# A four-layer graph kernel: the length-1 LSTM of 1024 tokens as seven block products, and the pieces of the neighbouring streams placed anew

## The chip, the cores and the metric

The kernel runs on one core of a Trainium2 chip. The metric is the device time of one launch in microseconds (us). An execution under the profiler gives the trace and the page that are read here. The engines are named as in the profile: PE (TensorE, matmuls), PEld (its weight loads), DVE (VectorE), ACT (ScalarE), POOL (GpSimd) and SP (SyncE, which only issues DMAs here). Each engine has its own instruction stream; they meet through semaphores.

## The reference, cut to what matters

128 graphs of 64 nodes with 256 channels go through four layers, each with a residual. The layer that matters here is the second: two graph convolutions, and then LSTMs over windows of the 64 nodes of length 1, 2, 3 and 4, one after the other, each of which writes the last state of every window back into `h`.

```python
h = relu(einsum('ts,bsh->bth', adj, x @ Wg0 + bg0))
h = relu(einsum('ts,bsh->bth', adj, h @ Wg1 + bg1))
for p in range(1, 5):
    nw = 64 // p
    wins = h[:, :nw * p].reshape(Bv * nw, p, 256)
    last = lstm_last(Wih[p - 1], Whh[p - 1], bih[p - 1], bhh[p - 1], wins)   # gates i, f, g, o; zero initial state
    h = h.at[:, arange(nw) * p + p - 1].set(last.reshape(Bv, nw, 256))
```

With length 1 every token is a window of its own. The state starts at zero, so the forget gate and `Whh` drop out: i, g and o are `x @ Wih.T + bias`, the cell is sigmoid(i) * tanh(g), the state sigmoid(o) * tanh(cell).

## The kernel before, in words

The 8192 tokens are 16 chunks of 512. Stage 1 and stage 2 (layer 1) go over the chunks; then comes the LSTM stage, then layers 3 and 4. The LSTM stage has 8 **rounds** (`sc`) of two chunks, so of 1024 tokens. The data of a round is `hT`, channels on the partitions: 2 blocks of 128 channels by 64 nodes by 16 graphs.

A matmul is [128 x 128] weights by [128 x n] data into one PSUM bank of 512 f32 per partition. During the LSTM stage there are 8 banks: two each of the tags x, y and z, and two (ps) for other work (`banks_of("psum1", x=2, y=2, z=2, ps=2)`).

`lstm(p, hv, sets, name)` (L1009) does one length. For p = 1 it is called twice a round with 512 tokens each: 3 gates x 2 channel blocks x 2 input blocks = 12 matmuls of 512 columns (L1123), weights `wih1`. ACT reads the banks directly (`first_acts`, L1102: sigmoid or tanh with bias), DVE multiplies the cell (`first_cell`, L1108) and writes the states (L1062). For p = 2 to 4 the first step is the same kind of product (L1123; for p = 2, in rounds 1 to 7, in two sets of 256 columns, since the two halves of the tokens become ready one after the other). The later steps are done per gate by **seven block products** instead of eight (class `Unit`, L1159): with the 2 x 2 blocks of the weights and the two halves of the tokens, kinds 1 to 7 are products of sums and differences, which are then added up. Sums of weights lie in the `wset` tiles, loaded from `wfar` in memory, where `weight_sums` put them during stage 2. Differences of the data are made by `differences` (L313 to L316), on POOL for the inputs (`xd`), on DVE for the states (`hd`). Kinds 1, 6, 7 and 4 add up in one x bank, each being read on the way: after kind 1 ACT copies the bank (L1165), only then may kind 6 be added into it. Kind 5 goes to a y bank and is copied too; kinds 2 and 3 go to z.

The order of the work is written out by hand: in the LSTM stage the program order is the order of the instructions on all five engines (`manual_schedule`). The LSTM is a Python generator that yields at 22 **places** in a round, 0 to 21, and at each place pieces of other streams are emitted:

- Places 0 to 3 lie in length 1, 4 to 7 in length 2, 8 to 13 in length 3, 14 to 21 in length 4. In lengths 2 to 4 the first place lies between the two input blocks of the first product, the second after the first products of the next step (kinds 5, 3, 2 from x) and just ahead of kind 5 from h, its copy, kind 1, its copy, kinds 3, 6, 2; then come two per step, in its middle and at its end. Place 17 is the end of a step of length 4 and, like place 9, lies just ahead of those products and copies.
- `convolutions(c)` (14 steps) prepares a chunk of the next round. Step 1: scale on DVE, two transposes on DVE, a put to memory, a read-back, and the load of x, on SP. Step 2: DVE adds the read-back to x. Step 3: `ln_stats`, eight DVE instructions (L159, L160) and, on POOL, a power (L99, L100). Steps 4 and 5: `apply_halves`, a shift on DVE (L194), then two relus on ACT (L196) in each step. Steps 6 to 14: an aggregate on PE (64 small matmuls, L214), copies (DVE), the v product (PE, L898), bound (DVE), the u product (PE, L912), bias (DVE), an aggregate (PE), and twice two relus into `hT` (ACT, L923).
- `residual(c)` (3 steps) for the round before: four transposes on DVE (L1269) and a put; a read-back; an addition on DVE.
- `ahead(c)` (6 steps): a put; a re-ordering read-back; statistics; shift and two relus; two relus; transposes on DVE and a put.

The tuples RESIDUAL, CONV, BEGUN, FIRST, AHEAD and LATE give the place of each step. CONV holds the two chunks of the next round in rounds 1 to 6, FIRST in round 0, BEGUN the steps that the first chunk of the round after the next has already had, in rounds 0 to 5; LATE the last steps of `ahead` for the second chunk, in the round after (from round 2 on).

Tiles lie in pools that are stacked in SBUF. A tile that comes to lie on bytes of closed pools waits for the users of the earlier tiles on its own bytes (`reuse_waits="tile"`). `early` (L1363), into which the x of the first two chunks is loaded at L930, is the first tile of pool l1, behind the pool w1 of the weights, and lies where the stage-2 pools lay.

Of the kernel before, what the change touches and what calls it, by code (L numbers as in the profile page):

```python
# [13 lines left out]
P = 128  # L14
# [5 lines left out]
def kernel(  # L20
# [304 lines left out]

    wqk_sb = const.tile([P, KD, D], F32, name="wqk_sb")
    wvo_sb = const.tile([P, KD, D], F32, name="wvo_sb")
# [362 lines left out]
    with tc.manual_schedule(engines={mybir.EngineType.PE}):  # L690
# [26 lines left out]

        def weight_products():
            for m in range(KD):
                ps = bank(f"c1_{m}")  # L720
                nc.tensor.matmul(ps[:, :P], bg0_sb[:, m * P : (m + 1) * P], adjt_bd, start=True,
                                 stop=True)
                nc.scalar.copy(c1[:, m, :], ps[:, :P])
                nc.scalar.mul(nc1[:, m, :], ps[:, :P], -1.0)
            for a in range(KD):
                for dst, lhs, rhs in ((wqk_sb, 0, wt[:, KD : 2 * KD, :]), (wvo_sb, 2 * KD, wo_sb)):
                    ps = bank(f"wp_{a}_{lhs}")
                    for f in range(KD):
                        nc.tensor.matmul(ps[:, :D], wt[:, lhs + f, a * P : (a + 1) * P],
                                         rhs[:, f, :], start=(f == 0), stop=(f == KD - 1))  # L730
                    nc.scalar.copy(dst[:, a, :], ps[:, :D])
            ps = bank("c2")
            for k in range(KD):
                nc.tensor.matmul(ps[:, :D], c1[:, k, :], wg1_st[:, k, :], start=(k == 0),
                                 stop=(k == KD - 1))
            return ps
# [3 lines left out]
        def weight_sums(p, q):  # L740
            w = stage.tile([P, 16, P], F32, tag="ws", name=f"ws_{p}_{q}", bufs=2)
            for i, src in enumerate((wih_t, whh_t)):
                nc.sync.dma_start(
                    w[:, 8 * i : 8 * i + 4, :].rearrange("p (k c) f -> p k (c f)", k=KD),
                    src[p - 1].rearrange("(k p) f -> p k f", p=P)[:, :, q * D : (q + 1) * D])
            yield
            v = w.rearrange("p (i b) f -> p i b f", i=2)
# [3 lines left out]
            far = dram.tile([P, 15, P], F32, tag=f"ws{p}{q}", name=f"wfar_{p}_{q}", bufs=1)  # L751
            nc.sync.dma_start(far[:, :9], w[:, :9])
            nc.sync.dma_start(far[:, 9:], w[:, 10:])
            wfar[p, q] = far
            yield

        wanted = [(p, q) for p in range(2, SKIP + 1) for q in GATES]
# [3 lines left out]
    with tc.manual_schedule(engines={mybir.EngineType.PE, mybir.EngineType.DVE,  # L761
# [3 lines left out]
        for c in range(2, NCH - 1):  # L765
            a, b, z = sevens[c], sevens.get(c + 1), sevens.get(c - 1)
            weights = weight_sums(*wanted.pop(0)) if wanted else None
            if weights:
                next(weights)
# [43 lines left out]
            if weights:  # L813
                next(weights)
# [43 lines left out]
    wih1 = w1.tile([P, KD, 3, D], F32, name="wih1")  # L858
    for i, q in enumerate(GATES[:3]):
        nc.sync.dma_start(wih1[:, :, i, :],  # L860
                          wih_t[0].rearrange("(k p) f -> p k f", p=P)[:, :, q * D : (q + 1) * D])
# [147 lines left out]
    def lstm(p, hv, sets, name):  # L1009
# [34 lines left out]
        hn = None if p == 1 else l1.tile([P, KD, CH], F32, tag="hs", name=f"hs_{name}", bufs=1)  # L1044
        hd = None if p == 1 else l1.tile([P, 4, CH // 2], F32, tag="hd", name=f"hd_{name}", bufs=1)
# [38 lines left out]
        if p > 1:  # L1084
            b = {(k, j): hn[:, k, halves[j]] for k in range(KD) for j in range(2)}
            dh = differences(nc.vector, [hd[:, i, :m] for i in range(4)], b[0, 0], b[0, 1], b[1, 0], b[1, 1])
            oh = {i: folded(a) for i, a in {1: b[0, 0], 2: b[1, 0], 3: b[1, 1], 4: hd[:, 3, :m],
                                            5: hd[:, 0, :m], 6: hd[:, 1, :m], 7: hd[:, 2, :m]}.items()}
            ox = {1: operands_x(1)}


        def block(q, c, k):
            if p == 1:
                return wih1[:, k, GATES.index(q), c * P : (c + 1) * P]
            return wsets[p, q][:, 2 * k + c, :]
# [15 lines left out]
        for i, w in enumerate(sets):  # L1111
            products = [(q, c, k) for q in GATES[:3] for c in range(KD) for k in range(KD)]
            if p > 1:

                products.sort(key=lambda o: o[2])
            for at, (q, c, k) in enumerate(products):
                if i == len(sets) - 1 and at == (8 if p == 1 else 6):
                    if p == 1:
                        first_acts(0, 2)
                        first_cell(0)  # L1120
                        first_cell(1)
                    yield
                nc.tensor.matmul(  # L1123
                    banks[q, c][:, :n].rearrange("p (w b) -> p w b", b=nb)[:, w, :], block(q, c, k),
                    hv[:, k, w.start * p : (w.stop - 1) * p + 1 : (w.step or 1) * p, :],
                    start=(k == 0), stop=(k == KD - 1))
        if p == 1:
            first_acts(3)
        else:
            first_acts(0, 2)  # L1130
            first_cell(0)
            first_acts(3)
            first_cell(1)
        for c in range(KD):
            new_state(0, c, every)
            if p > 1 and not c:
                dh[0]()
        if p > 1:
            dh[1]()
            dh[2]()  # L1140


# [58 lines left out]
        A = [Unit(q, 1) for q in (0, 2)] if p > 1 else []  # L1201
# [78 lines left out]

    def lstms(sc, hT):
        hv = hT.rearrange("p k (t b) -> p k t b", t=T)
        for p in range(1, SKIP + 1):
            if p > 1:
                parts = [hv]
            elif sc:
                parts = [hv[:, :, i * T // 2 : (i + 1) * T // 2, :] for i in range(2)]
            else:
                parts = [hv[:, :, :, i * NB : (i + 1) * NB] for i in range(SUP)]
            nw = parts[0].shape[2] // p  # L1290
            sets = [slice(0, nw)]
            if p == 2 and sc:
                sets = [slice(0, nw // 2), slice(nw // 2, nw)]
            for i, part in enumerate(parts):
                yield from lstm(p, part, sets, f"{sc}_{p}_{i}")
# [53 lines left out]
    RESIDUAL = (0, 2, 3), (1, 3, 5)  # L1349
    CONV = (1, 2, 3, 3, 4, 4, 5, 6, 7, 8, 9, 10, 10), (3, 5, 6, 7, 8, 11, 12, 13, 14, 15, 16, 17, 18, 20)  # L1350
    BEGUN = 20
    FIRST = (0, 2, 3, 4, 4, 5, 6, 7, 8, 9, 10, 11, 12, 12), (3, 6, 7, 8, 8, 13, 14, 15, 16, 17, 18, 19, 20, 20)
    AHEAD = (4, 5, 10, 12, 14, 18), (6, 7, 21)
    LATE = 1, 1, 3
# [23 lines left out]
    with tc.manual_schedule(engines={mybir.EngineType.PE, mybir.EngineType.DVE, mybir.EngineType.Pool,  # L1378
                                     mybir.EngineType.Activation, mybir.EngineType.SP}):
        last = NCH // SUP - 1  # L1380
        for sc in range(last + 1):
# [7 lines left out]
            if sc > 1:  # L1389
                units(LATE[:2], aheads[sc * SUP - 3])  # L1390
# [9 lines left out]
            if sc > 1:  # L1400
                units(LATE[2:], aheads[sc * SUP - 3])
# [3 lines left out]
            if sc + 1 < last:  # L1405
                units([BEGUN], convs[(sc + 2) * SUP])
# [17 lines left out]
    l2, close_l2 = pool("l2", 2)  # L1424
    w3_sb = w2p.tile([P, KD, 3 * D], F32, name="w3_sb")
# [518 lines left out]
```

## Time and profile before

| | |
|---|---|
| median of 3 runs | 1905.5 us (1904.4 to 1905.61) |
| the profiled execution, first to last instruction (span) | 1903.0 us, 2.5 us under the median; its launch time is not recorded by itself |
| PE | 15293 matmul records (two per matmul), no clock below full |
| LSTM stage | from about 272 us to 1530 us |
| one round, for example round 4 | 908.35 to 1069 us |
| first instructions of length 1 in it | 908.35 to 928.95 us on PE |

In the timeline of the trace, a line has the start in us, the busy time in us, the engine, the line of the kernel, the operation, output<-input with the shapes, the number of records that were merged (x), and in brackets the idle time ahead of it and what ended it. DMAs land some us after they are issued: the puts of `far_y` 2.2 to 10.0 us (median 2.8), the loads of x 3.9 to 7.4 us (median 4.7).

### The profile page before, as it was taken

The numbers are of one execution on the slowest core, as the hardware profiler recorded it, in microseconds if no ns is written. First come the engines' busy times: TensorE is split into PE (matmuls) and PEld (weight loads), VectorE is DVE, ScalarE is ACT, GpSimd is POOL, SyncE is SP. The second block draws the span as 40 slices with busy tenths as digits, with TensorE's granted clock in tenths as the row PEclk, the third lists the DMA queues.
The fourth block names the chain that finished last, engine by engine and source line by source line (L and its number), as shares of the span: only waits on it lengthen the run. The fifth ranks groups of instructions, "written<-read, shape, count | busy, mean of one in ns | idle before, by whom it ended". The sixth has DMA issues, their size and how long they took to land.

```text
span 1903.0 us, 39287 instructions
## 1 busy us (share of the span) xinstructions
PE 1879.9 (99%) x15293; PEld 1520.8 (80%) x15293; DVE 1201.7 (63%) x3093; ACT 980.6 (52%) x2212; POOL 499.7 (26%) x701
## 2 busy tenths in 40 slices
PE   8999999999999999999999999999999999999998
PEld 6877856896897898799689789878969967777776
DVE  6768844556557646655755755665555567767776
ACT  5766544445446455455554545545554544444453
POOL 5856611211211211121121121112112213233232
PEclk9999999999999999999999999999999999999999
DMA  3224643116324522531632452352144245444433
GB/s 114 79 67 149 234 163 108 75 43 205 117 84 161 183 84 96 189 102 53 220 113 84 162 181 84 115 178 107 53 148 128 92 134 156 134 144 146 142 115 112
DMA packets 110506, 240.42 MB, mean 126 GB/s; under 512 B 11377, under 2 KB 74353, under 8 KB 110321
## 3 DMA queue, kind: packets, MB, share of 16 engines
q1 hardware_dynamic: 109568, 236.57, 37.4%
q8 instruction: 121, 1.98, 0.4%
q0 software_dynamic: 320, 1.05, 0.2%
q14 instruction: 65, 0.52, 0.1%
q10 hardware_dynamic: 432, 0.30, 0.0%
HBM read 169.98 MB, written 67.90 MB: 125 GB/s over the span
## 4 chain that ended last, share of the span: by engine, by line
PE 90%; DVE 5%; ACT 2%; issue 1%; POOL 1%; DMA 1%; SPq 0%; DVEq 0%; ACTq 0%
PE x L1159 23%; PE g L1123 18%; PE z L1159 11%; PE y L1159 6%; PE v L1434 5%; PE u L912 3%; PE v L898 3%; PE p_q L1441 3%; PE X L1630 3%; PE X L426 2%; PE X L502 2%; PE Y L1630 1%; PE Y L426 1%; PE agg_c L214 1%; PE o L1757 1%
## 5 line engine op out<-in xcount | busy, mean ns | idle before, releaser
L1168 DVE TENSOR_TENSOR gates<-gates,x 128x128 f32<-128x128 f32 (+2 forms) x384 | 119.6, 323 | 334.8 <-PE x L1159 333.1
L1159 PE MATMUL x<-xd,wset 128*128 128x128 f32 (+2 forms) x1280 | 285.4, 311 | 0.2
L1159 PE MATMUL x<-hd,wset 128*128 128x128 f32 (+2 forms) x1152 | 247.0, 303 | 0.0
L1217 POOL TENSOR_TENSOR gates<-gates 128x512 f32<-128x512 f32 (+2 forms) x48 | 74.8, 1559 | 647.9 <-ACT gates L1051 647.9
L1159 PEld LDWEIGHTS x<-xd,wset 128*128 128x128 f32 x1280 | 202.2, 190 | 17.4 <-DVE gates L1168 3.8
L1051 ACT ACTIVATE gates<-gates,bias 128x256 f32<-128x256 f32 (+4 forms) x384 | 170.4, 491 | 67.2 <-DVE gates L1168 64.3
L1159 PEld LDWEIGHTS x<-hd,wset 128*128 128x128 f32 x1152 | 185.2, 191 | 4.9
L1102 ACT ACTIVATE gates<-g,bias 128x512 f32<-128x512 f32 (+2 forms) x240 | 138.0, 609 | 99.0 <-PE g L1123 95.6
L1123 PE MATMUL g<-hT,wset 128*128 128x256 f32 (+2 forms) x744 | 184.4, 405 | 1.1 <-DVE hT L1062 1.1
L1123 PEld LDWEIGHTS g<-hT,wset 128*128 128x128 f32 x744 | 140.8, 190 | 43.9 <-issue 8.8
L1123 PE MATMUL g<-hT,wih 128*128 128x512 f32 x384 | 166.5, 593 | 0.8 <-issue 0.8
L1165 ACT COPY gates<-y 128x128 f32<-128x128 f32 (+2 forms) x192 | 54.1, 293 | 205.4 <-PE y L1159 204.9
L1159 PE MATMUL z<-hs,wset 128*128 128x128 f32 (+2 forms) x768 | 154.2, 303 | 0.0
L1123 PEld LDWEIGHTS g<-hT,wih 128*128 128x128 f32 x384 | 72.4, 190 | 88.7 <-issue 84.3
L1159 PEld LDWEIGHTS z<-hs,wset 128*128 128x128 f32 x768 | 119.9, 191 | 3.3
L1108 DVE TENSOR_TENSOR cell<-gates 128x512 f32<-128x512 f32 (+2 forms) x80 | 50.3, 646 | 100.3 <-ACT gates L1102 100.2
L1168 DVE TENSOR_TENSOR gates<-gates,z 128x128 f32<-128x128 f32 (+2 forms) x384 | 104.8, 317 | 0.1
L1165 ACT COPY gates<-x 128x128 f32<-128x128 f32 (+2 forms) x192 | 56.4, 295 | 93.8 <-PE x L1159 93.1
L1051 ACT ACTIVATE gates<-x,bias 128x128 f32<-128x128 f32 (+2 forms) x192 | 74.7, 389 | 50.9 <-PE x L1159 48.0
L1159 PE MATMUL z<-hT,wset 128*128 128x128 f32 (+1 forms) x512 | 96.9, 302 | 0.0
L1159 PE MATMUL x<-hs,wset 128*128 128x128 f32 (+2 forms) x384 | 85.0, 303 | 0.0
L1228 ACT ACTIVATE gates<-cell 128x256 f32<-128x256 f32 (+2 forms) x144 | 55.3, 384 | 51.5 <-DVE cell L1227 51.0
(299 smaller groups left out, 3958.6 us busy)
## 6 DMA issues: line engine op xcount, KB each, us to landing
wset<-wfar SPq DMA_DIRECT2D x96, 960.0 KB, 6.5
hT<-far_h SPq DMA_DIRECT2D x124, 128.0 KB, 2.9
far_h<-hm SPq DMA_DIRECT2D x16, 512.0 KB, 4.4
far_n<-xs SPq DMA_DIRECT2D x16, 512.0 KB, 6.9
xs<-far_n SPq DMA_DIRECT2D x64, 128.0 KB, 2.9
far_x<-xs SPq DMA_DIRECT2D x16, 512.0 KB, 3.0
x<-far_x SPq DMA_DIRECT2D x64, 128.0 KB, 3.2
xt<-in_x_dram SPq DMA_DIRECT2D x15, 512.0 KB, 4.1
```

What stands on the lines that cost most here:

```text
L426: nc.tensor.matmul(self.banks[tag][:, i * CH // 2 : (i + 1) * CH // 2], w, self.at[kind], start=first and not i, stop=True, skip_group_che ...
L898: nc.tensor.matmul(banks[m], wg0_sb[:, k, m * P : (m + 1) * P], agg[:, k, :], start=(k == 0), stop=(k == KD - 1))
L912: nc.tensor.matmul(banks[j // 2][:, j % 2, :], v[:, k, j * P : (j + 1) * P], wg1_sb[:, k, :], start=(k == 0), stop=(k == KD - 1))
L1051: nc.scalar.activation(gate(q, c, part), src, AF.Tanh if q == 2 else AF.Sigmoid, bias=bs[:, q * KD + c : q * KD + c + 1])
L1102: nc.scalar.activation(columns_of(gate(q, c)), natural(banks[q, c][:, :n].rearrange("p (w b) -> p w b", b=nb)), AF.Tanh if q == 2 else AF. ...
L1123: nc.tensor.matmul(banks[q, c][:, :n].rearrange("p (w b) -> p w b", b=nb)[:, w, :], block(q, c, k), hv[:, k, w.start * p : (w.stop - 1) * ...
L1159: nc.tensor.matmul(folded(self.psum(kind)), wsets[p, self.q][:, BLOCKS[kind][i], :], (ox[self.s] if part == "x" else oh)[kind], start=firs ...
L1165: nc.scalar.copy(gate(self.q, kind // 5, halves[kind // 5]), self.psum(kind))
L1168: nc.vector.tensor_add(gate(self.q, *dst), gate(self.q, *a), self.psum(kind))
L1217: nc.gpsimd.tensor_mul(gates[:, 0, :, :n], gates[:, 0, :, :n], gates[:, 2, :, :n])
L1434: nc.tensor.matmul(ps[:, i, :], hT[:, k, j, :], w[:, k, first : first + D], start=(k == 0), stop=(k == KD - 1))
L1630: nc.tensor.matmul(st[c, tag][:, i * CH // 2 : (i + 1) * CH // 2].rearrange("p (a n) -> p a n", n=P), w, st[c, "o7"][kind], start=first an ...
```

## The change

It does four things.

1. Length 1 becomes `single(...)`: seven block products of 3 gates each over 1024 tokens (two of 512 tokens in round 0), 21 matmuls of 512 columns, in the six banks of x, y and z. ACT copies kinds 2, 5 and 6 out, DVE adds kinds 1, 3 and 7, kind 4 is read directly; POOL makes four differences of the data and two of the cells. The weights with their sums (`wih1`, now 3 x 7 blocks) come from memory, where `weight_sums` has put them.
2. The first product of length 2 is one set of 12 matmuls of 512 columns.
3. The products wqk and wvo for layer 3 no longer stay in SBUF: they are written over `wqkv_sb`, put to memory, and loaded again behind the LSTM stage.
4. The steps of the other streams get new places.

The core of the diff:

```diff
-    wqk_sb = const.tile([P, KD, D], F32, name="wqk_sb")
-    wvo_sb = const.tile([P, KD, D], F32, name="wvo_sb")
...
+        products = [wqkv_sb[:, :, i * D : (i + 1) * D] for i in range(2)]
+        products_far = dram.tile([P, KD, 2 * D], F32, tag="wqv", name="wqv_far", bufs=1)
...
                     nc.scalar.copy(dst[:, a, :], ps[:, :D])
+            nc.sync.dma_start(products_far, wqkv_sb[:, :, : 2 * D])
...
+            if p == 1:
+                for i, (_, q) in enumerate(sources):
+                    far = dram.tile([P, 7, P], F32, tag=f"ws{p}{q}", name=f"wfar_{p}_{q}", bufs=1)
+                    nc.sync.dma_start(far[:, :1], w[:, 8 * i : 8 * i + 1])
+                    nc.sync.dma_start(far[:, 1:], w[:, 8 * i + 2 : 8 * i + 8])
+                    wfar[p, q] = far
...
-        wanted = [(p, q) for p in range(2, SKIP + 1) for q in GATES]
+        wanted = [(p, (wih_t, q), (whh_t, q)) for p in range(2, SKIP + 1) for q in GATES]
+        wanted[6:6] = [(1, (wih_t, GATES[0]), (wih_t, GATES[1]))]
+        wanted[7:7] = [(1, (wih_t, GATES[2]))]
...
-    wih1 = w1.tile([P, KD, 3, D], F32, name="wih1")
+    wih1 = w1.tile([P, 3, 7, P], F32, name="wih1")
     for i, q in enumerate(GATES[:3]):
-        nc.sync.dma_start(wih1[:, :, i, :],
-                          wih_t[0].rearrange("(k p) f -> p k f", p=P)[:, :, q * D : (q + 1) * D])
+        nc.sync.dma_start(wih1[:, i], wfar[1, q])
...
+        products = [(q, c, k) for k in range(KD) for q in GATES[:3] for c in range(KD)]
+        for at, (q, c, k) in enumerate(products):
+            if at == 6:
+                yield
+            nc.tensor.matmul(
+                banks[q, c][:, :n].rearrange("p (w b) -> p w b", b=nb), wsets[p, q][:, 2 * k + c, :],
+                hv[:, k, : (nw - 1) * p + 1 : p, :], start=(k == 0), stop=(k == KD - 1))
...
+    def single(b, m, name, yields):
...
+        t = []
+        for i in range(4 * m // (2 * CH)):
+            part = l1.tile([P, 7 * (T // 3) * NB], F32, tag="xd", name=f"xd_{name}_{i}", bufs=2)
+            t += [folded(part[:, a : a + m]) for a in range(0, 2 * CH, m)]
+        for f in differences(nc.gpsimd, t, b[0, 0], b[0, 1], b[1, 0], b[1, 1]):
+            f()
+        right = {1: b[0, 0], 2: b[1, 0], 3: b[1, 1], 4: t[3], 5: t[0], 6: t[1], 7: t[2]}
+        ys, xs_ = [[bank(f"{n}_{name}_{g}", tag) for g, tag in enumerate(tags)]
+                   for n, tags in (("y1", "yyz"), ("x1", "zxx"))]
...
+        def product(kind):
+            for g in range(3):
+                nc.tensor.matmul(folded(ps(g, kind)), wih1[:, g, KINDS1[kind], :], right[kind],
+                                 start=kind in (2, 5, 1), stop=True, skip_group_check=True)
...
+        product(2)
+        copy((0, 0), 2)
+        product(1)
+        add((0, 0), 1)
+        for g in range(3):
+            act(g, 0, 0)
+        cell(nc.gpsimd, 0, 0)
+        if 0 in yields:
+            yield
+        product(5)
+        copy((1, 1), 5)
+        tanh(0, 0)
+        product(6)
+        copy((0, 1), 6)
+        state(0, 0)
+        if 1 in yields:
+            yield
+        product(3)
+        add((0, 1), 3)
+        for g in range(3):
+            act(g, 0, 1)
+        cell(nc.gpsimd, 0, 1)
+        product(7)
+        add((1, 1), 7)
+        act(0, 1, 1)
+        tanh(0, 1)
+        act(1, 1, 1)
+        act(2, 1, 1)
+        state(0, 1)
+        cell(nc.vector, 1, 1)
+        if 2 in yields:
+            yield
+        product(4)
+        act(0, 1, 0, ps(0, 4))
+        tanh(1, 1)
+        act(1, 1, 0, ps(1, 4))
+        act(2, 1, 0, ps(2, 4))
+        cell(nc.vector, 1, 0)
+        tanh(1, 0)
+        state(1, 1)
+        state(1, 0)
...
-    RESIDUAL = (0, 2, 3), (1, 3, 5)
-    CONV = (1, 2, 3, 3, 4, 4, 5, 6, 7, 8, 9, 10, 10), (3, 5, 6, 7, 8, 11, 12, 13, 14, 15, 16, 17, 18, 20)
-    BEGUN = 20
+    RESIDUAL = (0, 3, 4), (2, 5, 6)
+    CONV = (4, 4, 5, 6, 7, 8, 9, 10, 10), (6, 8, 9, 9, 10, 11, 12, 13, 14, 15, 16, 17, 18, 20)
+    BEGUN = 13, 15, 16, 17, 18
     FIRST = (0, 2, 3, 4, 4, 5, 6, 7, 8, 9, 10, 11, 12, 12), (3, 6, 7, 8, 8, 13, 14, 15, 16, 17, 18, 19, 20, 20)
-    AHEAD = (4, 5, 10, 12, 14, 18), (6, 7, 21)
-    LATE = 1, 1, 3
+    AHEAD = (4, 5, 10, 12, 14, 18), (6, 7)
+    LATE = 4, 5, 6, 7
...
+    wqv_sb = w2p.tile([P, KD, 2 * D], F32, name="wqv_sb")
+    nc.sync.dma_start(wqv_sb, products_far)
+    wqk_sb, wvo_sb = wqv_sb[:, :, :D], wqv_sb[:, :, D:]
```

Before, CONV's first tuple has 13 entries, for steps 2 to 14, since BEGUN held step 1 alone; after, BEGUN holds steps 1 to 5 and the tuple 9 entries, for steps 6 to 14. The second tuple has all 14 steps in both versions: steps 1 to 5 stood at 3, 5, 6, 7, 8 and stand at 6, 8, 9, 9, 10.

## The prediction

> **What bounds the kernel now.** I read the page first, its busy shares and its chain of work:
>
> ```profile
> PE 1879.9 (99%) x15293; PEld 1520.8 (80%) x15293; DVE 1201.7 (63%) x3093; ACT 980.6 (52%) x2212; POOL 499.7 (26%) x701
> PEclk9999999999999999999999999999999999999999
> ...
> PE 90%; DVE 5%; ACT 2%; issue 1%; POOL 1%; DMA 1%; SPq 0%; DVEq 0%; ACTq 0%
> ```
>
> TensorE (PE) is busy 1879.9 of 1903.0 us, so all its waits together are 23 us. In the busy times by stretch, round 4 (908.35 to 1069 us) has 160.62 us of PE in 160.65: whatever is taken from PE there is won, and whatever makes it wait is lost. Then the timeline of PE at the start of that round:
>
> ```profile
> 908.35 20.77 PE L1123 MATMUL g<-hT,wih 128*128 128x512 f32 x48
> 928.95 7.93 PE L1123 MATMUL g<-hT,wset 128*128 128x256 f32 x36
> 936.82 1.16 PE L214 MATMUL agg_b<-adjt_bd,cv 64*64 64x64 f32 x64
> 937.91 2.86 PE L1123 MATMUL g<-hT,wset 128*128 128x256 f32 x12
> 940.60 1.03 PE L1159 MATMUL y<-xd,wset 128*128 128x256 f32 x4
> ```
>
> A matmul leaves two records. The length-1 LSTM is 24 matmuls from 908.35 to 928.95: 20.60 us, 0.858 each. The start of length 2 is 24 of half the width: 7.87 + 2.69 = 10.56 us.
>
> **What is won.** Length 1 becomes 21 matmuls of the same width: 21 x 0.858 = 18.02, so 2.58 us less in each of rounds 1 to 7: 18.1 us. Length 2 starts with 12 matmuls of 512 columns; round 0 has that form already (294.90 to 305.31, 10.41 us), so 0.15 us less, or 0.26 by 12 x 0.858; I take 0.2, times 7: 1.4. Round 0 has two products of 256 columns: 42 x 0.437 (7.87/18) = 18.4 against 24 x 0.858 = 20.6, 2.2 less; but ScalarE (ACT) then has 25 instructions per product, 9 copies of 0.37, 12 gates of 0.47, 4 tanh of 0.42 (rows of 256 columns): 10.7 us against PE's 9.2, so there it can also be 1 us slower. I take 0.5 less. Won: 18.1 + 1.4 + 0.5 = 20.0 us.
>
> **The new length-1 code itself is covered in rounds 1 to 7.** Per round, ACT has 25 instructions of some 0.60 us (four of L1102 in a row took 2.42): 15.0 us of 18.0. VectorE (DVE) has 15 of 0.65 (9.8) and the eight transposes of the residual (2 x 2.1): 14.0. GpSimd (POOL) has six of about 1.3 (1.27 is a 512-element row of L1217): 7.8. Laid on round 4's rows: product kind 2 at 908.35, its copies from 911.82, where ACT's first gates wait now for the last state of length 4; kind 5, which overwrites those banks, is due at 913.5 and the first bank is free at 912.4. The last states come at 929.9, and length 2 needs them at 932.6, behind six matmuls and the aggregate. If this cover fails, each microsecond costs seven.
>
> **What is lost: pieces that now stand in front of ACT's copies.** Step 3 of a convolution is statistics on DVE and a power on POOL; step 4 a shift on DVE and two relus on ACT. For the second chunk, step 3 goes from place 6 to 9 and step 4 from 7 to 9. Place 9 is in length 3, just ahead of the copies of block products 5 and 1, and PE adds product 6 into the bank that copy 1 must have read. PE, then ACT, then DVE, around place 9:
>
> ```profile
> 980.25 1.16 PE L214 MATMUL agg_c<-adjt_bd,cv 64*64 64x64 f32 x64
> 981.34 0.84 PE L1159 MATMUL y<-hd,wset 128*128 128x168 f32 x4
> ...
> 983.72 0.73 PE L1159 MATMUL x<-xd,wset 128*128 128x168 f32 x4
> ```
> ```profile
> 981.93 0.58 ACT L1165 COPY gates<-y 128x168 f32<-128x168 f32 x2 [1.82 <-PE y L1159]
> 982.78 0.30 ACT L1165 COPY gates<-x 128x168 f32<-128x168 f32 x1 [0.27 <-PE x L1159]
> ```
> ```profile
> 981.29 0.33 DVE L316 TENSOR_TENSOR hd<-hs,hd 128x168 f32<-128x168 f32 x1
> ```
>
> Copy 1 ends at 983.08; PE takes the bank at 983.72: 0.64 us of slack. In the new order DVE begins the statistics at 981.62, behind L316. They take 2.22 (988.16 to 990.38, the same eight instructions), the power on POOL with its waits 1.45 (913.85 to 915.30), the shift 0.16 to 0.2, two relus 1.05 (1010.16, 1.09 with its tail), the three copies 0.86: 981.62 + 2.22 + 1.45 + 0.2 + 1.05 + 0.86 = 987.4. PE waits 987.45 - 983.72 = 3.7 to 3.8 us; only the aggregate (1.1 us) stands in front, and it is there already. ACT keeps its order even where a later instruction could run; at place 1 now:
>
> ```profile
> 920.38 2.08 ACT L196 ACTIVATE h<-xs,nmr_n,rstd_n 128x256 f32<-128x256 f32 x4 [0.83 <-DVE nmr_n L194]
> 922.36 1.24 ACT L1102 ACTIVATE gates<-g,bias 128x512 f32<-128x512 f32 x2
> ```
>
> The first of those two gates had its bank at about 920.4 (918.65 + 2 x 0.858); it ran behind the four relus, which had idled 0.83 us for their shift. Behind the new relus are queued the four copies, and PE waits for those. Bounds: 3.4 with every gap at its smallest, 4.9 with the slowest such chain (the last statistics of the other stream end at 929.27, its relus begin at 932.21: 2.9 instead of 1.65). A wait below zero has no reason: PE has nothing else to do there. Rounds 1 to 6 have it: 6 x 3.8 = 22.8 us.
>
> **Place 17** gets step 4 of the chunk begun early, again ahead of the copies. Its statistics (place 16) are done, but its shift is queued on DVE behind L316, which ends at 1042.86: 1043.02 + 1.05 + 0.67 (copies of 0.20, 0.20, 0.27) = 1044.75, and PE's product 6 is due at 1042.90: 1.85 us (2.4 if the shift takes the 0.69 it took at 931.48; 1.7 at least). Round 0 is covered: there a u product (3.5 us) lies at place 17. Rounds 1 to 5: 5 x 1.85 = 9.3 us. **Place 18** gets step 5, two relus, 1.05 us, ahead of the gates at 1051.20, where ACT had idled only 0.19: the gates come 0.86 later, and by cell, tanh, state and difference the first hd, done at 1053.93 now, at 1054.8; PE wants it at 1054.28 (as 1041.01 stands to 1043.84, so this to 1057.11). 0.55 us, between 0 and 0.9: 5 x 0.55 = 2.8.
>
> The other moved pieces I cost at nothing. Statistics at place 4 lie on DVE while PE does twelve matmuls of length 2; relus at 5 and the squares at 7 lie beside the v and u products (3.5 us each); step 1 at place 6 (2.3 us of DVE, with its neighbours 4.8) fits between 956.66 and 964.16; step 2 at 8 fits ahead of the cells at 977.52. SP's queue: the put of step 1 at 6 goes out behind two weight loads, like the put at 904.23, whose read-back came at 912.45, so 8.2 us later, about 968.6, and its data are there at 975.5, for a place at 976. At 15 it is close: put at 1020, read-back 1022.7, x at 1024.4 + 4.1 = 1028.5, the sum until 1029.8 for adds due at 1029.71, with 0.8 us of slack on PE behind that. If one of these comes late, it is 0.5 to 1 us a round.
>
> **The start of the LSTM.** The old wqk/wvo products now overwrite wqkv_sb and are put to memory before it is given up. By the sizes in the code, the tile `early` moves 1152 elements up (wih1 grows from 1536 to 2688) and covers the whole of wqkv_sb; now it covers 384 elements of it. So the x loads of the first two chunks must wait for that put. ACT and SP now:
>
> ```profile
> 243.88 0.37 ACT L731 COPY wvo_sb<-wp 128x256 f32<-128x256 f32 x1 [0.49 <-PE wp L729]
> ```
> ```profile
> 236.41 0.92 SPq L930 DMA_DIRECT2D early<-in_x_dram x2
> ```
>
> The put can start at 244.3, lands after 2.8 us (median of such puts), and x 4.1 to 4.7 us after that, about 251.4; DVE wants it at 245.77 (L941), on the chain. 5.6 us lost; 0 if the tiles lie otherwise, 10 if the loads of small weights (4.6 us of SP) also stand behind the put. The page's clock row is full throughout and PE's longest wait in the list of waits is 2.7 us, so no row shows what PE does after a longer idle. [...]
>
> **Sum.** -20.0 + 22.8 + 9.3 + 2.8 + 5.6 = +20.5 us on a span of 1903.0: 1923.5. The median of the runs is 1905.5, 2.5 above the span; with that 1926.0 us, 1.1% slower. The bounds of the terms give 1905.5 - 22 + 20 + 8.5 = 1912 to 1905.5 - 19 + 29 + 12 + 4.5 + 10 = 1942.
>
> **Rivals.** (1) *Faster*: the relus at places 9 and 17 don't hold the copies. It decides at the 0.64 us of slack at 983.72: if statistics, power, shift and relus were through by 982.4, PE would not wait. That needs DVE to reach place 9 some 4 us earlier against PE than now, or another order on ACT. For it: DVE and ACT are half idle in length 3. Against: the difference L316 that DVE has to finish first hangs on the same PE products. Price: -20.0 + 5.6 = 1891, or 1885.5 without the wait at the start. (2) *Only place 9 counts*, and half as much (1.9 us): -20 + 11.4 + 5.6 = about 1902.5, within or just below no change. (3) *Length 1 bound by its evictions*: ACT at 15.0 of 18.0 us, with relus or waits added, sets the pace and PE's time there stays near 20.6: then the 18.1 are not won, 1944. Against it: the states end 2.7 us ahead of need in my layout. (4) The change wins no PE time at all: excluded, the matmuls are counted in the code.
>
> **Chances.** Forecast with its bounds, 1912 to 1942: 0.62. Rival 1: 0.26. Rival 2: 0.07, mostly inside 0.2%. Rival 3: 0.05. About 0.2% (3.8 us) is what a measurement of this kernel can tell from no change. Faster 0.27, within 0.05, slower 0.68. The range for 8 in 10 reaches into rival 1, to 1890, and ends at 1938, which leaves out the cheaper half of rival 1 and the dearest sums; the forecast's own range is 1912 to 1938.
>
> **What would show it.** Right: the products with wih at 294 records of 512 columns and 84 of 256, about 18.0 us a round; in PE's waits, `x L1159 <- ACT gates L1165` with some 30 us in a dozen waits, the longest near 3.8, each behind agg_c in length 3; ACT's L196 ahead of L1165 there, waiting for nmr_b; xs L941 waiting some 5 us for early. Wrong: PE at 99% with no such waits (rival 1), or idle inside the wih group (rival 3).

## The result, and the profile after

The changed kernel takes 1966.5 us (median; 1961.1 to 1969.3), the kernel before 1904.95: ratio 1.032, 95% interval 1.0305 to 1.0335. Slower, as forecast, but by 61.5 us instead of 20.5, and outside the range. The profiled execution has a span of 1964.6 us, 61.6 more than before; all differences below are against 1903.0. The four runs spread over 8 us, the fastest with a mean granted clock of 0.996 and the slowest with 0.989, so what is put down to the clock below holds for the profiled run (0.992).

The page of the changed kernel, the lines that answer to those of before: busy PE, the granted clock in 40 slices, the chain's shares by engine.

```profile
PE 1879.6 (96%) x15119; PEld 1494.1 (76%) x15119; DVE 1263.7 (64%) x3164; ACT 1015.8 (52%) x2309; POOL 567.9 (29%) x763
PEclk9999989999999999999999999999999999999999
PE 69%; DVE 9%; ACT 5%; DMA 2%; issue 2%; POOL 1%; SPq 0%; DVEq 0%; ACTq 0%; POOLq 0%
```

PE has 174 records fewer and is busy just as long, with 85 us of idle instead of 23; the chain now runs through DVE, ACT and DMAs for 16% of its way, 8% before. The list of PE's waits (what PE was held by: us in total, times, longest):

```profile
PE x L1149 <- ACT gates L1155: 27.8, 11, 3.3
PE at_b L239 <- ACT cv L892: 10.1, 1, 10.1
PE x L1149 <- DVE gates L1158: 9.5, 13, 2.1
PE x L1304 <- ACT gates L1063: 6.3, 7, 0.9
```

The first row is the prediction's: 6 x 3.28 at place 9 and 5 x 1.61 at place 17. The others it had small or not at all.

**Where the 61.6 us are**, from the first matmul of length 1 in each round (before to after): the LSTM starts at 291.8 instead of 272.7 us, +19.1. Round 0 takes 165.0 instead of 161.8, +3.1. Rounds 1 to 3 are 9.1, 8.7 and 7.2 longer, rounds 4 and 5 6.0 each, round 6 3.5; round 7 is 1.2 shorter. Behind the LSTM nothing changes.

**Place 9 in round 4**: PE, then DVE, then ACT. The text in brackets is idle time and what ended it.

```profile
1029.36 0.73 PE L1149 MATMUL z<-hs,wset 128*128 128x168 f32 x4
1033.37 0.84 PE L1149 MATMUL x<-xd,wset 128*128 128x168 f32 x4 [3.28 <-ACT gates L1155]
```
```profile
1027.17 0.33 DVE L316 TENSOR_TENSOR hd<-hs,hd 128x168 f32<-128x168 f32 x1
...
1031.12 0.49 DVE L194 SCALAR_TENSOR_TENSOR nmr_b<-mv_b,rstd_b 128x4 f32<-128x4 f32 x1 [1.48 <-POOL rstd_b L100]
```
```profile
1031.64 1.09 ACT L196 ACTIVATE cv<-xs,nmr_b,rstd_b 128x256 f32<-128x256 f32 x2 [5.66 <-DVE nmr_b L194]
1032.64 0.47 ACT L1155 COPY gates<-y 128x168 f32<-128x168 f32 x2
1033.01 0.51 ACT L1155 COPY gates<-x 128x168 f32<-128x168 f32 x2
```

This is the predicted chain, link by link: statistics behind L316, the power on POOL, the shift, two relus, and only then the copies, although their products had been done for some 3 to 4 us.

**Length 1 in round 4** on PE, then the cells of length 4 on DVE and the differences on POOL beside them:

```profile
958.13 1.88 PE L1304 MATMUL x<-hT,wih 128*128 128x512 f32 x4
960.91 1.13 PE L1304 MATMUL x<-hT,wih 128*128 128x512 f32 x2 [0.90 <-ACT gates L1063]
962.27 2.81 PE L1304 MATMUL y<-xd,wih 128*128 128x512 f32 x6 [0.23 <-ACT gates L1324]
```
```profile
955.27 0.42 DVE L1216 TENSOR_TENSOR cell<-cell,gates 128x256 f32<-128x256 f32 x1
955.80 1.38 DVE L1217 TENSOR_TENSOR cell<-cell,gates 128x256 f32<-128x256 f32 x1
957.67 0.93 DVE L1074 TENSOR_TENSOR hT<-gates 128x256 f32<-128x256 f32 x1 [0.48 <-ACT gates L1218]
958.52 1.35 DVE L1216 TENSOR_TENSOR cell<-cell,gates 128x128 f32<-128x128 f32 x1
```
```profile
955.64 1.27 POOL L314 TENSOR_TENSOR xd<-hT 128x512 f32<-128x512 f32 x1 [1.07 <-PE x L1149]
956.86 1.45 POOL L315 TENSOR_TENSOR xd<-hT,xd 128x512 f32<-128x512 f32 x1
958.39 1.33 POOL L316 TENSOR_TENSOR xd<-hT,xd 128x512 f32<-128x512 f32 x1
```

Length 1 takes 19.67 us, not 18.02. The same DVE form takes 0.42 us at 955.27 and 1.38 half a microsecond later, and each of the three slow ones ends 0.15 to 0.3 us behind the POOL operation that it overlaps. So the last state of length 4 ends 5.9 us after the start of length 1, and the copies begin there; the bank that PE waits for 0.90 us is read by a gate of length 4 (ACT L1063) that waits for these cells.

**The start**: POOL, then ACT, then SP's queue. L754 are the weight sums; the line with `sc_bn` begins the power of the batch norm at the end of stage 2, which stood at 237.96 before.

```profile
243.12 2.90 POOL L754 TENSOR_TENSOR ws<-ws 128x256 f32<-128x256 f32 x4 [6.32 <-DMA ws<-in_whh_t_dram]
245.99 0.22 POOL L99 TENSOR_SCALAR sc_bn<-mv_bn 128x1 f32<-128x1 f32 x1
```
```profile
248.88 1.21 ACT L732 COPY wqkv_sb<-wp 128x256 f32<-128x256 f32 x4
259.46 2.23 ACT L892 ACTIVATE cv<-z1a,sh_bn,sc_bn 128x512 f32<-128x512 f32 x3 [9.38 <-DMA wqv_far<-wqkv_sb]
```
```profile
251.47 0.60 SPq L733 DMA_DIRECT2D wqv_far<-wqkv_sb  x1
259.50 0.94 SPq L942 DMA_DIRECT2D early<-in_x_dram  x2
```

The products are ready at 250.1 instead of 244.3 (stage 2 is 5.5 us late), the put goes out behind the small loads, and it lands 7.9 us later. The scaled chunk `cv` waits for it as well as `early`. DVE has `early` at 263.6; the sum had 251.4.

### The profile page after: what moved, and what is told of

Read it like the earlier page. It is cut to its first block, busy times and chain, and to the rows that moved or that the text cites. A ratio compares the mean times of both kernels' runs of the same rounds, so it can differ in the third digit from the quotient of the medians.

```text
span 1964.6 us, 39217 instructions
## 1 busy us (share of the span) xinstructions
PE 1879.6 (96%) x15119; PEld 1494.1 (76%) x15119; DVE 1263.7 (64%) x3164; ACT 1015.8 (52%) x2309; POOL 567.9 (29%) x763
## 4 chain that ended last, share of the span: by engine, by line
PE 69%; DVE 9%; ACT 5%; DMA 2%; issue 2%; POOL 1%; SPq 0%; DVEq 0%; ACTq 0%; POOLq 0%
PE x L1149 19%; PE z L1149 9%; PE g L1120 8%; PE v L1530 5%; PE y L1149 5%; PE x L1304 3%; PE p_q L1537 3%; PE u L924 3%; PE v L910 3%; PE X L1726 2%; PE y L1304 2%; DVE cell L1217 1%; DVE cell L1216 1%; PE Y L1726 1%; DVE gates L1158 1%
## 5 line engine op out<-in xcount | busy, mean ns | idle before, releaser
L1063 ACT ACTIVATE gates<-gates,bias 128x256 f32<-128x256 f32 (+4 forms) x384 | 169.9, 490 | 61.7 <-DVE gates L1158 59.3
L1120 PEld LDWEIGHTS g<-hT,wset 128*128 128x128 f32 x576 | 108.5, 190 | 70.0 <-issue 39.5
L1107 ACT ACTIVATE gates<-g,bias 128x512 f32<-128x512 f32 (+2 forms) x144 | 76.9, 562 | 67.8 <-PE g L1120 67.3
L1063 ACT ACTIVATE gates<-x,bias 128x128 f32<-128x128 f32 (+2 forms) x192 | 74.8, 390 | 50.2 <-PE x L1149 47.4
L313 POOL TENSOR_TENSOR xd<-hT 128x128 f32<-128x128 f32 (+3 forms) x57 | 38.4, 674 | 160.0 <-DVE hT L1074 100.5
L1149 PE MATMUL y<-hd,wset 128*128 128x128 f32 (+2 forms) x384 | 81.2, 314 | 0.0
L1149 PE MATMUL y<-xd,wset 128*128 128x128 f32 (+2 forms) x384 | 78.6, 307 | 2.1 <-ACT gates L1107 2.1
```

Of the source, the lines that this page charges most:

```text
L1063: nc.scalar.activation(gate(q, c, part), src, AF.Tanh if q == 2 else AF.Sigmoid, bias=bs[:, q * KD + c : q * KD + c + 1])
L1107: nc.scalar.activation(columns_of(gate(q, c)), natural(banks[q, c][:, :n].rearrange("p (w b) -> p w b", b=nb)), AF.Tanh if q == 2 else AF. ...
L1120: nc.tensor.matmul(banks[q, c][:, :n].rearrange("p (w b) -> p w b", b=nb), wsets[p, q][:, 2 * k + c, :], hv[:, k, : (nw - 1) * p + 1 : p, ...
L1149: nc.tensor.matmul(folded(self.psum(kind)), wsets[p, self.q][:, BLOCKS[kind][i], :], (ox[self.s] if part == "x" else oh)[kind], start=firs ...
```

## The experiments

Theory: the loss is the start, the pieces at places 9, 10, 17 and 18 with a lower clock behind the first, and POOL beside DVE in length 1. Rivals: the new code of length 1 is itself the loss; or the placements are. Medians are given; the kernel before has 1904.0 to 1904.7 in these series. Line numbers are each kernel's own.

**1. The code without the placements**, and **2. the placements without the code.** The diff of the first restores the five tuples (and which steps of LATE are issued first at their places); that of the second sets them in the kernel before.

```diff
-    RESIDUAL = (0, 3, 4), (2, 5, 6)
-    CONV = (4, 4, 5, 6, 7, 8, 9, 10, 10), (6, 8, 9, 9, 10, 11, 12, 13, 14, 15, 16, 17, 18, 20)
-    BEGUN = 13, 15, 16, 17, 18
+    RESIDUAL = (0, 2, 3), (1, 3, 5)
+    CONV = (1, 2, 3, 3, 4, 4, 5, 6, 7, 8, 9, 10, 10), (3, 5, 6, 7, 8, 11, 12, 13, 14, 15, 16, 17, 18, 20)
+    BEGUN = 20,
...
-    AHEAD = (4, 5, 10, 12, 14, 18), (6, 7)
-    LATE = 4, 5, 6, 7
+    AHEAD = (4, 5, 10, 12, 14, 18), (6, 7, 21)
+    LATE = 1, 1, 3
```

> The changed kernel with the places of the kernel before (RESIDUAL, CONV, BEGUN, AHEAD, LATE); the new length 1, the new first product of length 2, the weight sums and the stage-2 tiles stay as changed. Theory (the loss is the start, 19 us, and the pieces that were placed ahead of copies at places 9, 17, 18 and 10, with the lower clock behind them): these waits go, some 20 + 8 + 3 + 5 us, and up to 9 us of clock, so about 1966 - 40 = 1926 us, and more, up to 1945, if the eight relus and the statistics that then lie in length 1 again hold the new code's copies there (ACT has 15 us of its own in 18 us, with four relus 19). Rival (the new code of length 1 is the loss, the places are harmless): 1960 us or more.

> The kernel before with the places of the changed kernel, nothing else. Theory: the same waits of some 3.3 us at place 9, 1.6 at 17, 0.4 at 18 and 0.9 at 10 appear although length 1 is the old code, 30 to 36 us in all, and the lower clock behind place 9 adds up to 9: 1935 to 1950 us. Rival (the places are harmless, the new code is the loss): 1905 us, within 4.

Measured: 1949.2 us (ratio 1.0235, 1.022 to 1.0251) and 1955.6 us (1.0273, 1.0258 to 1.0289), each above its theory's range by 4 to 6 us and further from its rival's. The placements alone cost 52 us in the old code: PE's waits are 28.7 us for copies and 8.1 for gates, with 3.27, 0.86, 1.64 and 0.43 us at places 9, 10, 17 and 18 of round 4, and the mean clock is 0.994. The code alone costs 45, of which 18 are the start; its rounds lose 17.6 us (six times 2.9) to a new wait, of kind 5 for POOL's difference, which is queued behind the power of the statistics at place 21. There POOL starts its other differences late. Neither half is free as it stands, and the halves don't add up: each meets another queue.

**3. The products in a tile of their own**, and **4. also no extra weight sums in stage 2.**

```diff
+        wprod.append(stage.tile([P, KD, 2 * D], F32, name="wprod"))
-            nc.sync.dma_start(products_far, wqkv_sb[:, :, : 2 * D])
+            nc.sync.dma_start(products_far, wprod[0])
...
-        wanted[6:6] = [(1, (wih_t, GATES[0]), (wih_t, GATES[1]))]
-        wanted[7:7] = [(1, (wih_t, GATES[2]))]
+                nc.gpsimd.tensor_tensor(dst, a, b, op)
```

(The last line stands in a loop over four sums in `wih1`, 3 gates at once, among the steps of the first convolutions.)

> The changed kernel, but the products wqk and wvo lie in a tile of their own at the end of the stage pool instead of over wqkv_sb; their put and the later load stay. Theory (the tiles of the x loads and of the first scaled chunk waited for that put because they lie on its bytes): the 10.1 us wait of at_b falls to 1 or 2 us, 8 to 9 us less, with the clock 1 to 3 more: 1954 to 1959 us. Rival (the start waits for the late weight sums and the late bn power alone): 1966 us, within 2, with a wait as long for the x loads behind the small loads.

> As the run with the products in their own tile, and the sums of the length-1 weights are not made in stage 2: the blocks are loaded straight into wih1 and four wide operations of POOL add them up ahead of the LSTM, where POOL is idle. Theory (the other 5.5 us at the end of stage 2 are the extra weight sums, whose loads hold POOL, behind which the differences of stage 2 and the bn power are queued): length 1 of round 0 starts within 2 us of the 272.7 us of before, in all 17 to 20 us less than the changed kernel: 1946 to 1950 us. Rival (the sums are harmless, POOL being a quarter busy): as the run with the tile alone.

Measured: 1966.3 us (1.0316, 1.029 to 1.0343) and 1951.5 us (1.0246, 1.0231 to 1.0261). The first missed: `cv` no longer waits, but the x loads are still queued on SP behind the put, and the put behind weight-sum puts that POOL delays to 247; DVE waits 9.25 us for `early` and PE 9.85 at the next step. The LSTM starts 3.6 us earlier; the rounds give 2.3 of it back (mean clock of the execution 0.991), and the rest is lost behind them. With the sums out of stage 2 the LSTM starts at 276.8, 15.0 earlier than in the changed kernel. Taken away in this order the overlaid bytes are worth 3.6 us and the weight sums, through POOL's and SP's order, 11.4; taking the sums alone away was not tried.

**5. Another order of POOL's differences** (on top of 4), t[0] and t[1] first, the others behind the first cell:

```diff
-        for f in differences(nc.gpsimd, t, b[0, 0], b[0, 1], b[1, 0], b[1, 1]):
-            f()
+        nc.gpsimd.tensor_tensor(t[0], b[0, 1], b[0, 0], OP.subtract)
+        nc.gpsimd.tensor_tensor(t[1], b[1, 1], t[0], OP.subtract)
...
         cell(nc.gpsimd, 0, 0)
+        nc.gpsimd.tensor_tensor(t[2], b[1, 1], b[0, 1], OP.subtract)
+        nc.gpsimd.tensor_tensor(t[3], b[1, 0], t[1], OP.subtract)
```

> As the run with the tile and the sums (1951.5 us), and in length 1 POOL makes the differences in another order: those for kinds 5 and 6 first, those for kinds 7 and 4 behind the first cell. Theory (three 512-wide POOL operations beside DVE's last cells of length 4 stretch these from some 0.4 to 0.9 to 1.4 us, so the last state comes 2.5 us later and the first copies with it): the cells take 0.3 to 0.45 us again, the waits of 0.9 and 0.2 us inside length 1 go, 1.1 to 1.6 us less in each of rounds 1 to 7: 1940 to 1944 us. Rival (length 1 is bound by its own evictions): within 2 us of 1951.5, the waits stay or move to a later product.

Measured: 1945.8 us (1.0215, 1.02 to 1.0231), 5.8 less. POOL is through at 935.85, the later cells take 0.28 to 0.43 us, and length 1 takes 18.02 or 18.03 us in every one of rounds 1 to 7, without a wait. That is 11.5 us, of which about half was lost again: the clock now falls in all of rounds 1 to 6 (four matmul records of 168 columns behind the wait at place 9 take 1.33 us instead of 0.73, at 520.41, 685.31, 849.22, 1012.94, 1176.71 and 1340.32 us; mean clock 0.993, in run 4 0.997), and the LSTM starts 1.4 us later. In rounds 1 to 7 its own evictions don't bind length 1.

**6. The old RESIDUAL, CONV and BEGUN on top of 5**; AHEAD and LATE stay new.

> As the run with the other order of differences, and RESIDUAL, CONV and BEGUN have their places of the kernel before; AHEAD and LATE keep the new ones, so that no statistics stand at place 21 ahead of length 1. Theory (the placements at 9, 10, 17 and 18 are the loss of the rounds, and with the old places only the power at place 21 hurt the new code): the waits for copies and gates go, some 35 us, with the clock 4 to 8 more: 1895 to 1906 us, rounds 1 to 6 at 155 to 157 us. Rival (the new length 1 can't carry these pieces: 19 us of ACT and 17.5 of DVE in 18 us): waits of 1 to 3 us appear in length 1 of every round, 1915 to 1930 us.

Measured: 1922.3 us (1.0089, 1.0074 to 1.0105): a miss, the rival's range. In round 4 PE waits 1.20 us in length 1, where the second residual's transposes and step 2 of the convolution (both at place 1) stand ahead of DVE's additions, and 2.04 at place 5, where the new LATE and the old RESIDUAL meet:

```profile
960.05 1.29 DVE L284 TENSOR_TENSOR xs<-xs,hT 128x512 f32<-128x512 f32 x2 [1.48 <-DMA hT<-far_h]
961.26 0.15 DVE L194 SCALAR_TENSOR_TENSOR nmr_n<-mv_n,rstd_n 128x4 f32<-128x4 f32 x1
```

The 0.15 us shift that ACT's relus and copies need is queued behind an addition that waits for its DMA.

**7. Place 9 alone, in the kernel before**, and **8. the same with PE kept busy there.**

```diff
-    CONV = (1, 2, 3, 3, 4, 4, 5, 6, 7, 8, 9, 10, 10), (3, 5, 6, 7, 8, 11, 12, 13, 14, 15, 16, 17, 18, 20)
+    CONV = (1, 2, 3, 3, 4, 4, 5, 6, 7, 8, 9, 10, 10), (3, 5, 9, 9, 10, 11, 12, 13, 14, 15, 16, 17, 18, 20)
...
+                if 0 < sc < last and n == 9:
+                    keep_busy(24, f"p{sc}")
```

> The kernel before with steps 3, 4 and 5 of the second chunk alone at places 9, 9 and 10 (6, 7 and 8 before). Theory: a wait of 3.3 to 3.8 us at place 9 and 0.9 at place 10 in each of rounds 1 to 6, 25 to 28 us; if the clock drops behind the wait as it did in the changed kernel, up to 10 us more: 1929 to 1942 us. Rival (place 9 hurts only together with the other moved pieces): 1905 to 1915 us.

> As the run before it, and in rounds 1 to 6 TensorE has 24 extra transposes, some 2.9 us, at place 9 ahead of the aggregate, so that it is busy while the statistics, the power and the relus run, and doesn't wait long. The output is the same. If what a round loses beyond its waits is the clock that drops after a wait of over 3 us: the granted clock stays at 1.00, and the kernel with the extra work is as fast as or up to 10 us faster than without it (1928 to 1934 us). If it isn't the clock: as slow, or slower by what of the filling is not hidden, up to 6 x 2.9 = 17 us.

Measured: 1942.2 us (1.0197, 1.0182 to 1.0213) and 1931.8 us (1.0142, 1.0125 to 1.0159): 10.4 us faster with more work. Three steps of one chunk cost 37 us: six waits of 3.27 and six of 0.86 are 24.8, and most of the rest is clock (mean of the execution 0.994). Busy times in 4 us stretches around the wait that ends at 841.33, first without, then with the filling (the second number after the stretch is PE's busy time; the last three are the granted clock, the DMA share and GB/s):

```profile
836.00:840.00 4.00, 2.07 (x15) 1.81 (x13) 2.00 (x8) 0.39 (x1) 2.21 (x4) 1.00 0.01 4
840.00:844.00 4.00, 2.67 (x9) 2.67 (x10) 0.33 (x1) 1.48 (x6) 1.89 (x6) 0.60 0.00 0
```
```profile
836.00:840.00 4.00, 3.46 (x25) 3.20 (x24) 0.50 (x1) 1.87 (x6) 3.59 (x8) 1.00 0.00 0
840.00:844.00 4.00, 4.00 (x31) 4.00 (x30) 2.59 (x9) 2.12 (x6) 0.00 (x0) 1.00 0.01 2
```

Here 24 transposes fill 2.7 us of PE that were idle; the wait is 0.54 us, and the mean clock of the execution is 1.000. Waits and filling together are as long as the waits were (24.6 and 24.8 us in six rounds), so the 10.4 us are the clock's.

**9 and 10. Other places** on top of 5; the second also issues the put from ACT's queue.

```diff
 # 9
+    CONV = (4, 4, 5, 6, 7, 8, 9, 10, 10), (3, 6, 7, 8, 8, 11, 12, 13, 14, 15, 16, 17, 18, 20)
 # 10
+    CONV = (2, 3, 4, 4, 5, 6, 7, 8, 9, 10, 10), (3, 6, 7, 8, 8, 11, 12, 13, 14, 15, 16, 17, 18, 20)
+    BEGUN = 13, 15, 16
+            nc.scalar.dma_start(products_far, wprod[0])
```

> As the run with the other order of differences (1945.8 us), and of the second chunk steps 1 to 5 stand at 3, 6, 7, 8 and 8 instead of 6, 8, 9, 9 and 10; BEGUN stays at 13 to 18. Theory: the waits at places 9 (3.3) and 10 (0.9) and the clock behind the first go, 25 us with about 6 of clock, in rounds 1 to 6: 1914 to 1921 us; the waits of 1.6 at place 17 and 0.4 at 18 stay in rounds 1 to 5. Rival (four relus at place 8 hold the first gates of length 3, or the loss is in BEGUN): 1930 us or more.

> As the run before it, and BEGUN holds steps 1 to 3 alone, at 13, 15 and 16; steps 4 and 5 stand at places 2 and 3 of the next round; the put of the products is issued by ACT instead of SP, so that the x loads on SP don't stand behind it. Theory (every loss of the changed kernel is then taken away): length 1 of round 0 starts at 272.5 to 274 us, 4 us earlier; the waits at 17 and 18 go; rounds 1 to 6 take 155.2 to 156.5 us (157.8 before, 2.6 less at best): 1888 to 1898 us, faster than the kernel before. Rival (the new code of length 1 wins nothing even without waits): 1904 us or more.

Measured: 1978.3 us (1.0389, 1.0375 to 1.0404) and 1972.2 us (1.036, 1.0346 to 1.0374), both misses, and worse than the change. In the second the start is mended (274.1 us, 4.2 earlier than in the first), but in both DVE comes late from place 4 on and PE then waits for its difference `hd`, in the second 44.4 us in seven waits, up to 8.2. SP's queue and DVE in round 4 of the second:

```profile
973.21 1.74 SPq L254 DMA_DIRECT2D cv<-far_y  x4
...
975.52 1.87 SPq L254 DMA_DIRECT2D hT<-far_h  x4
```
```profile
981.82 1.29 DVE L284 TENSOR_TENSOR xs<-xs,hT 128x512 f32<-128x512 f32 x2 [8.00 <-DMA hT<-far_h]
```

The residual's read-back from `far_h`, put there at place 0, is issued behind the convolution's read-back at the same place 3, which waits for its own put; DVE waits at the addition for 8 us, the cells and PE behind it. At place 8 four relus cost another 1.9 us.

**11 and 12. The same with those two put right**; in 12 the core of it is

```diff
+    RESIDUAL = (0, 3, 4), (2, 5, 7)
+    CONV = (2, 3, 4, 4, 5, 6, 7, 8, 9, 10, 10), (3, 5, 6, 7, 8, 11, 12, 13, 14, 15, 16, 17, 18, 20)
+    BEGUN = (14, 16, 18), (13, 15, 16)
+    AHEAD = (4, 5, 10, 12, 14, 18), (8, 9)
+    LATE = 4, 5, 6, 7
```

with LATE and the first residual issued ahead of the convolutions at a place; 11 has RESIDUAL (0, 2, 4) and one BEGUN.

> The two runs before it lost 6.6 to 8.2 us a round at place 4, where the addition of the residual waited for a read-back that SP held behind another put's read-back issued first at the same place 3, and 2 us at place 8 behind four relus. Here the read-back of the first residual stands at place 2, the second residual's addition at 7, steps 1 to 5 of the second chunk at 3, 5, 6, 7 and 8, AHEAD's second chunk at 8 and 9, and the LATE steps come first at their places; start, tile, sums and order of differences as mended. Theory (no piece then stands ahead of what PE waits for): rounds 1 to 6 at 155.2 to 157 us, clock 1.00: 1888 to 1899 us. Rival (the pieces moved out of length 1 find no free place elsewhere): a new wait of 1 us or more a round in length 2 or 3, 1904 us or more.

> As the run before it, with three repairs: the first residual's read-back stands at place 3 again, but is issued ahead of the convolution's step there, and behind the transposes of the second residual, whose data it overwrites; in the last round the second residual's addition stays at 6, ahead of the put that reads it; and in round 0 BEGUN stands at 14, 16 and 18, since at 13 its DVE work made PE wait 2.1 us there. Theory (with every piece off the paths that PE waits for, the seven products win what was worked out for them, 2.6 us a round): rounds 1 to 6 at 155.2 us, clock 1.00, round 0 at 163 to 165: 1889 to 1896 us. Rival (the read-back at place 3 or the repaired order brings a wait of 1 us or more a round): 1902 us or more.

Measured: 1895.8 us (0.9954, 0.994 to 0.9967) and **1892.8 us (0.9937, 0.9923 to 0.995)**, faster than both kernels. (In 11 the first residual's read-back overwrites data that the second still has to read, and in the last round a put reads rows ahead of their addition, so those values are not the reference's; the amount of work is the same.) Rounds 2 and 3 of 12 take 155.2 us, 2.7 to 2.9 less than before, at a clock of 1.00 (mean of the execution 0.998); round 0 takes 163.2. Against the profile before, rounds 1 to 7 are 17.5 us shorter in all; the start is 2.7, round 0 1.4 and the part behind the LSTM 2.3 longer (the cause of the last is not shown). PE in length 1 of round 4:

```profile
905.12 2.74 PE L1294 MATMUL y<-hT,wih 128*128 128x512 f32 x6
907.70 2.74 PE L1294 MATMUL x<-hT,wih 128*128 128x512 f32 x6
910.28 2.74 PE L1294 MATMUL y<-xd,wih 128*128 128x512 f32 x6
```

## Why the prediction was right and wrong

- **Right: the pieces ahead of the copies.** Place 9: 3.28 us for 3.8. Place 17: 1.61 for 1.85. Place 18: 0.43 for 0.55. Together 29.9 us for 34.9; run 2 shows them without the new code, run 7 the first alone. The chain is as long as worked out (5.9 us from the first statistic to PE's next product, 5.8 in the sum); DVE comes to it 0.4 us earlier against PE. The other pieces that were costed at nothing show no wait in rounds 1 to 6, but for place 10.
- **Wrong, the largest: the start, 19.1 us for 5.6** (bounds 0 to 10). The step followed the overlaid tile from the end of the products and took that end, and 2.8 us for the put, as given. But the extra `weight_sums` stand on POOL and SP ahead of stage 2's differences and of the batch norm's power, and the put stands behind their late puts and the small loads. Link by link: the products are ready 5.8 us later than in the sum, the put is issued 1.4 behind them, and it takes 7.9 us to land instead of 2.8: 12.3 of the 13.5 us that are missing. Run 4 takes 15.0 of the 19.1 away, and with the put on another queue (run 10) the LSTM starts at 274.1, 1.4 behind the kernel before. Also `cv` overlaps `wqkv_sb`, and PE's clock is 0.50 from 253.4 to 263.7 and from 270.5 to 273.9 us.
- **Wrong: "the new length-1 code itself is covered".** Won were 0.93 us a round, not 2.58: 6.4 instead of 18.1. The layout took DVE's cells at their old lengths beside new 512-wide POOL work. Run 5 moves that work and gives 18.02 us, the predicted time, so the count of PE and ACT was right; what POOL's operations do to DVE's cells was left out: beside them the three slow operations of DVE take 0.93 to 1.38 us and end 0.15 to 0.3 us behind POOL's, where run 5 has 0.28 to 0.43.
- **Wrong: place 10 at nothing.** Step 5's relus hold the gates there: 0.86 us in each of six rounds, 5.2. **Round 0**: +3.1 instead of -0.5; 2.08 are the first step of BEGUN at place 13, which stands on DVE ahead of an addition PE waits for, and 0.95 is length 1 in halves of 256 columns, with waits for ACT and DVE inside it, as the other bound had it.
- **Wrong: the clock left out of the sum.** Rounds 1 to 3 are 7.3 us longer than three rounds like 4 and 5 with the same waits, at 0.98 and 0.99. Run 8, in which PE is kept busy at place 9, has a mean clock of 1.000, run 7 0.994: it is the idle PE that lowers the clock. In the kernel before PE waits for 2.7 us at most, and the clock is full until after PE's last matmul (0.50 only from 1901.7 us on), so no wait there showed it. Waits of 3.27 us lower the clock in all six rounds of run 7, to 0.50 for 3.4 or 6.8 us at a time.
- Sum: 20.5 predicted; +13.5 start, +11.7 length 1, +1.0 length 2 (won 0.06 a round, not 0.2), +3.6 round 0, +5.2 place 10, +7.3 clock, -5.0 shorter waits: 57.8 of 61.6. The remaining 3.8 are some 0.6 us a round, perhaps in part slower first matmuls behind a wait (0.84 us for 0.73 at 1033.37); that was not tried by itself.

Of the rivals, the one that ended faster failed where it was said to decide: the relus were through at 1032.64, 4 us too late. The one in which place 9 alone counts, with 1.9 us, fails by 3.28 there and by the other waits. The one bound by evictions has most of its 18.1 us (11.7 were not won), but not its cause: in run 5, with the same evictions, length 1 takes 18.03.

## What to carry to other kernels

When a step is moved in a hand-written order, write down for each engine and for the DMA queue what stands behind it at the new place, and cost every one; each of runs 1 to 10 lost time to an instruction that was ready but queued behind one that wasn't. Work added to an idle engine isn't free if it shares a queue with work on the path, or stretches that work by running beside it (here DVE's cells, from 0.42 us to 1.38): cost the preparing stage and its loads too. And a saving on a bound engine is had only when all new waits are gone: the 2.6 us a round stood in length 1 as soon as POOL's order was mended (run 5), but made the kernel faster only once the start and the places were mended too.

## What the runs showed of the hardware

- PE's granted clock falls to 0.50 around the end of a wait of about 3.3 us: in the changed kernel for 6.8, 6.8 and 3.4 us in rounds 1 to 3, from 2.0, 2.4 and 3.0 us after PE has stopped; in run 7 for 3.4 us in five rounds and 6.8 in one (round 5); in round 4 of run 2 the matmuls slow down 4.7 us after the stop. Not every such wait does it: six of six in runs 5 and 7, rounds 1 to 3 and not 4 to 6 in the changed kernel. Waits near 2 us go either way: behind 2.18 us (run 6, 616.67) the clock fell (four matmul records of 512 columns took 3.65 us instead of 1.88), behind 2.04 us (run 6, 963.48) and 2.08 us (the changed kernel, 418.43) it didn't; no wait of 1.60 to 1.71 us in runs 5 and 6 and the changed kernel did it. Filling the idle time with 2.7 us of useless transposes made the kernel 10.4 us faster (run 8 against run 7).
- Operations of DVE on the cells and states of length 4 took 0.93 to 1.38 us in the changed kernel beside a 512-wide POOL operation, and ended 0.15 to 0.3 us behind it; in run 5, without it, the cells and states there take 0.28 to 0.43. The one cell of run 5 that still overlaps (935.22) takes 0.92.
- The put of 512 KB to `wqv_far` in the changed kernel took 7.9 us to land (251.47 to 259.4). The fourteen puts of `far_y` before, of the same size, took up to 10.0 us, with a median of 2.7; the 2.2 and 2.8 given for them ahead of the prediction count the read-backs in.
